# New orders for the steps of a two-layer graph attention kernel, with twelve instead of ten of a cycle's output sums on VectorE

## The chip, the core and the metric

The kernel runs on one core of one Trainium2 chip. The core has five engines that work at the same time, each through its own queue of instructions in order: TensorE (PE in the profile: matmuls, with PEld for the loading of the stationary operand), VectorE (DVE), ScalarE (ACT), GpSimd (POOL) and SyncE (SP, which here issues the DMA transfers). The metric is the device time of one execution in microseconds (us); the time of a kernel is the median over its runs.

## The reference

All data is float32: `x` is 128 batches x 128 agents x 512 features, `adj` is 128 batches x 128 x 128, zeros and ones. Two layers follow one another, each with a residual and a layer norm.

```python
def _L0_gnn_ref(inputs, adj, Wq, bq, Wk, bk, Wv, bv, Wo, bo):   # 8 heads of 64
    q = (inputs @ Wq + bq).reshape(bs, n, N_HEADS, HEAD_DIM)     # k and v likewise
    logits = jnp.einsum('bqhd,bkhd->bhqk', q, k) / np.sqrt(HEAD_DIM)
    logits = jnp.where((adj > 0)[:, None, :, :], logits, NEG_INF)
    attn = jax.nn.softmax(logits, axis=-1)
    out = jnp.einsum('bhqk,bkhd->bqhd', attn, v).reshape(bs, n, EMBED_DIM)
    return jax.nn.relu(out @ Wo + bo)

def _L1_gnn_ref(h, W, a, adj):
    Wh = jnp.matmul(h, W)
    e = _leaky((Wh @ a1)[:, :, None] + (Wh @ a2)[:, None, :])
    e = jnp.where(adj > 0, e, -9e15)
    attention = jax.nn.softmax(e, axis=1)
    return _leaky(jnp.einsum('bij,bjf->bif', attention, Wh))

x = _layernorm(x + _L0_gnn_ref(x, adj, ...))
x = _layernorm(x + _L1_gnn_ref(x, W1, a, adj))
```

## The kernel before

**Products.** The 512 x 512 products are done by the scheme of Strassen and Winograd: seven products of quarter-size blocks (`p1` to `p7`) in place of eight, with sums of blocks before and after (`strassen`, with the order of its pieces in `ORDER`). The projections to Q, K and V work on a group of four batches and use the scheme twice, nested. Each of the three is done in two *rounds*, one for each part of the inner scheme: an even round with four inner products, an odd round with three. Six rounds make a group (`c % 6`: 0 and 1 for Q, 2 and 3 for K, 4 and 5 for V). The products of layer 0 with Wo and of layer 1 with W1 work on a pair of batches and use the scheme once. W1 carries a 257th column for the edge scores.

**Orders.** No scheduler chooses the order of instructions. Under `tc.manual_schedule` every engine gets its instructions in the order in which the Python code issues them, and that order is written out as lists of tokens: `BEGIN` for the first six batches, four lists in `STEADY` for batch step t = 6 to 123 (the list t % 4), and `PLAN` for the end. A token names a step; its instructions are appended to the queues of the engines that it uses. A queue runs strictly in order, and each instruction waits at the head of its queue until its inputs are there and its output buffer is free. So the lists fix what stands behind what on each engine, while the order between engines comes from the data. SP issues all transfers of the steady part, also in list order, and an issue takes some 0.48 us on SP in the trace.

A steady list's token is a job, a dot and a step of it. The jobs:

- `f` and `s`: the softmax of layer 0 for two batches. `scores` (PE, L874), `add` (the mask, DVE L888), `reduce` (row maxima, DVE L897), `exp.i.j` (heads i and j, ACT L908), `reciprocals` (DVE L918), `divide` (ACT L922), `store` and `fetch` (the probabilities go to DRAM and come back with 32 x 32 blocks in place, L929 and L935, into `paz`), `transpose` (DVE L941, `pa<-paz`), `attend` (PE L954, `p_oT`), `copy` (ACT L969), `sum.n` (POOL L522 to L525). Both batches of a pair have their scores in an even list and attend in the odd list after it.
- `z`: layer 0's product with Wo for a pair, `p1` to `p7` (PE L800), `t0`, `t2`, `t3` (ACT copies, L811), `by`, `bw` (bias copies into the PSUM bank, ACT L821), `c11`, `c12` (DVE L1058), `c22` (DVE, a first add at L1062 and a residual at L1046), `c21` (L1046), `stats` (DVE L1002, L1004), `rstd` (POOL L1008, L1010), `apply` (DVE L1023), `store` (L1082). `g` and `p` are the same pair one and two lists later: `apply`, `store`, `fetch_both`, `transpose` (DVE L425) and `sum.n` (POOL).
- `w`: layer 1's product with W1 for a pair (PE L800, 257 columns wide), with its copies (ACT L811, and L1143 for `c21`) and adds (DVE L1145).
- `e`, `n`, `v`: layer 1's edges. `v.senders`, `v.store`, `v.fetch` send the outer sums through DRAM (L1176, L1251, L1261); `e.turn_blocks` (DVE L1186), `e.add` (ACT L1190), `e.maxima` (DVE L1196), `e.exp` (ACT L1200), `e.divide` (DVE L1204, L1205), `e.product` (PE L1210), `e.copy` (ACT L1217). One list later the batch is `n`: `residual` (DVE L1220), `stats`, `rstd`, `apply`, `store`.
- `m`: `masks`, `cast` (ACT L849), `mask` (DVE L852), `residuals` (L447), `x_pair` and `x_one` (loads of x, L420), `turn` (its 32 x 32 transposes, DVE L425), `sum.n` (the outer sums of x for the next group, POOL L522 to L525).

Tokens without a job are steps of the projections, and take the next one due:

- `h`: one outer product of a round, four or three matmuls (`split_step`, matmuls at L680). It queues up what reads its PSUM bank.
- `a`: the next of those copies, ACT (`copy_out`, L693, L696, L699). `d`: the next of those adds, DVE (L714).
- `k`: the next of the sums that finish a round (`combine`, the add at L730), on POOL; `k.v`: the same on VectorE.
- `i.s1a` to `i.s4b`: a sum of the inner scheme on x, on POOL, with `.v` on VectorE (L499).
- `q`: the load of the next weight block into a ring of four (`fetch_until`, L633).

Tiles with one buffer tie steps together: `paz`, the cells of a round, the three PSUM banks of the projections (`st_y`, `st_w`, `st_x`) and the five banks that all other products share. This loop runs the lists:

```python
        for token in STEADY[t % GROUP].split():
            if not common(token, g if t % GROUP else g + 1):
                name, method, *numbers = token.split(".")
                getattr(jobs[name], method)(*map(int, numbers))
```

Of the kernel before, what the change touches and what calls it, by code (L numbers as in the profile page):

```python
# [23 lines left out]
    y.order.3 y.q.0.0 y.order.2 b0.masks y.q.1.0 y.rows.2 y.rows.3 b4.load.1 b6.load.0  # L24
    b5.load.2 w.bias b2.masks y.q.2.0 y.q.2.1 y.q.1.1 y.oq.1 y.k.3 y.k.1 y.k.2 b4.turn
    b1.cast y.q.3.0 y.q.0.1 b0.cast y.oq.2 b7.load.1 y.q.3.1 b1.mask wk.build.0 b6.turn
    b5.turn wk.build.1 b3.cast b0.mask wk.build.2 wk.build.3 y.ok.2 b2.cast wq.scale.0
    y.oq.0 wq.scale.1 wq.scale.2 y.ok.1 y.ok.3 wq.scale.3 wk.build.4 wk.build.5 y.k.0 y.ok.0
    y.oq.3 s0.scores wk.build.6 b7.turn wk.build.7 b2.mask b3.mask s1.scores g1.0 g1.2
    b9.load.0 b8.load.2 w.halve wq.build.0 wq.build.1 wk.store.0 wq.build.2 s0.add.1  # L30
    s0.add.0 g1.1 i1.s1b b4.masks s0.reduce s1.add.0 s1.add.1 i1.s2b g1.3 wk.store.1
    s0.exp.0.1 s0.exp.6.7 b4.cast s0.exp.4.5 i1.s1a.v wk.store.2 y.v.1 wk.store.3 s0.exp.2.3
    b5.cast q q y.v.0 y.v.2 y.v.3 i1.s3a.v s1.reduce wq.build.4 s0.reciprocals.0
    s0.reciprocals.1 s0.divide.4.5 s0.divide.2.3 i1.s2a wq.build.3 i1.s4a.v wq.build.5
    s1.exp.5.6 s0.divide.0.1 h s1.exp.7 s1.exp.3.4 s0.divide.6.7 y.ov.0 s1.exp.0.1 y.ov.2
# [12 lines left out]
    s1.attend h g2.2 k h z0.p1 d w.w1_sum.2 k.v s1.copy a s3.reciprocals.1 d s1.sum.0
    s1.sum.2 h h z0.p2 b5.mask w.w1_sum.0 s1.sum.1 s3.exp.0.1 a z1.bw a b6.cast z0.t0
    s3.reciprocals.0 h z0.p6 h s3.divide.3.4 s3.divide.7 d w.w1_sum.1 s3.divide.5.6 z0.t2  # L50
    s3.divide.0.1 s3.divide.2 a h z0.p7 z0.p5 h q s2.fetch q w.w1_sum.3 w.block.3 w.w1_sum.6
# [14 lines left out]
    z0.transpose.1 d s5.transpose h h h z1.c12 z1.stats.0 z1.apply.1 d b13.load.0  # L66
    w.w1_block.0 i2.s4b w.w1_block.1 q q h s5.attend z1.rstd.0 z0.sum.0 a a s4.copy s5.copy
    z0.sum.1 z0.sum.2 w.w1_block.2 k w.w1_block.3 z0.sum.3 s5.sum.0 s5.sum.2 s5.sum.1 k k
    s5.sum.3 b13.turn z1.store.1
"""  # L70

STEADY = {
# [95 lines left out]
def kernel(  # L168
# [155 lines left out]
    wk = Weights(late)  # L324
# [1430 lines left out]
```

## Time and profile before

| | |
|---|---|
| median of 3 runs | 2299.22 us (2293.2, 2299.22, 2300.85) |
| the profiled execution: time, span | 2296.74 us, 2295.0 us |
| mean granted PE clock | 0.997 |
| PE busy | 2250.2 us, 98% |
| DVE busy | 2031.0 us, 89% |
| ACT busy | 1654.5 us, 72% |
| POOL busy | 1538.4 us, 67% |
| DMA | 540.80 MB, mean 236 GB/s |

The span is the profiled execution's time from its first to its last event, and its own time lies 1.74 us above it. A share is the busy time of an engine by the span; the shares of engines overlap. A row of waits names the engine and line that waited, the engine and line that released it, the sum, the times and the longest. In the timelines a start is in microseconds from the start of the span, and an idle time ahead of a row stands in brackets with its releaser. The steady lists run from about 174.5 us to 2199.5 us. Steps of the next stage are already mixed in at both ends.

### The profile page before, as it was taken

How to read it: one execution, taken by the hardware profiler on the slowest of the kernel's cores; microseconds unless marked ns; L12 is line 12 of the kernel's file. 1: busy time of each engine (PE TensorE's matmuls, PEld its weight loads, DVE VectorE, ACT ScalarE, POOL GpSimd, SP SyncE). 2: the span in 40 equal slices, each digit the busy share in tenths (PEclk: the TensorE clock that was granted, in tenths of full speed). 3: DMA queues.
4: the chain of work that ended last, by engine and by line, in shares of the span. 5: the costliest groups of instructions: out<-in, count | busy, mean ns of one | idle time of the engine just before them, and what ended most of it. 6: DMA issues, size and time to landing. Idle time of an engine off the chain costs nothing.

```text
span 2295.0 us, 52710 instructions
## 1 busy us (share of the span) xinstructions
PE 2250.2 (98%) x17228; PEld 2015.3 (88%) x17228; DVE 2031.0 (89%) x4140; ACT 1654.5 (72%) x5955; POOL 1538.4 (67%) x1782
## 2 busy tenths in 40 slices
PE   9999999999999999999999999999999999999998
PEld 5888998898898999998988998989898989888885
DVE  5879999999999999999999898999899998989877
ACT  3757677687676786776776777877767767768786
POOL 2656766667776677676667666677666776666656
PEclk9999999999999999999999999999999999999999
DMA  8977888788888888787878888778878888877764
GB/s 231 279 203 231 239 240 246 237 236 238 237 239 248 240 234 241 238 249 243 234 234 248 234 245 243 237 239 239 236 247 233 237 240 243 242 238 232 220 212 143
DMA packets 516594, 540.80 MB, mean 236 GB/s; under 512 B 100568, under 2 KB 394336, under 8 KB 516320
## 3 DMA queue, kind: packets, MB, share of 16 engines
q1 hardware_dynamic: 516000, 537.17, 79.4%
q8 instruction: 137, 2.24, 0.4%
q14 instruction: 137, 1.12, 0.2%
q10 hardware_dynamic: 320, 0.26, 0.0%
HBM read 388.96 MB, written 148.31 MB: 234 GB/s over the span
## 4 chain that ended last, share of the span: by engine, by line
PE 58%; DVE 17%; POOL 8%; DMA 8%; ACT 3%; issue 2%; SPq 2%; DVEq 0%; POOLq 0%; ACTq 0%
PE st_y L680 19%; PE p_y L800 13%; PE st_w L680 8%; PE p_w L800 7%; PE st_x L680 4%; DMA paz<-pa_dram 3%; DVE nmax L897 3%; DVE pa L888 3%; PE p_h L1210 2%; PE p_x L800 2%; POOL out_Q L730 2%; POOL rstd L1010 2%; POOL out_K L730 2%; PE lg L874 2%; ACT pa L908 1%
## 5 line engine op out<-in xcount | busy, mean ns | idle before, releaser
L908 ACT ACTIVATE pa<-pa,nmax 128x128 f32<-128x128 f32 x1000 | 391.9, 397 | 52.8 <-DVE nmax L897 51.8
L922 ACT ACTIVATE pa<-pa,rs 128x128 f32<-128x128 f32 x1000 | 326.6, 395 | 1.8 <-DVE rs L918 1.8
L969 ACT ACTIVATE arena<-p_oT,b_cols 128x128 f32<-128x128 f32 x504 | 141.2, 382 | 155.2 <-PE p_oT L954 155.1
L524 POOL TENSOR_TENSOR x1S<-x1T 128x256 f32<-128x256 f32 x62 | 48.7, 786 | 245.6 <-PE st_y L680 237.3
L1010 POOL TENSOR_TENSOR rstd<-ve,mhalf 128x1 f32<-128x1 f32 x256 | 189.7, 741 | 21.3
L693 ACT COPY cells<-st_y 128x384 f32<-128x384 f32 x279 | 132.6, 475 | 86.9 <-PE st_y L680 70.8
L908 ACT ACTIVATION_READ_ACCUMULATOR pa<-pa,nmax 128x1 f32 x1000 | 192.9, 193 | 0.0
L941 DVE STREAM_TRANSPOSE pa<-paz 128x1024 f32<-128x1024 f32 x125 | 154.8, 1238 | 19.3 <-DMA paz<-pa_dram 12.4
L1002 DVE BATCH_NORM_STATS2 st<-arena 128x6 f32<-128x512 f32 x248 | 168.8, 681 | 1.2
L888 DVE TENSOR_TENSOR pa<-lg,mf 128x512 f32<-128x512 f32 x250 | 164.3, 678 | 5.7 <-PE lg L874 5.7
L1008 POOL TENSOR_SCALAR ve<-mv 128x1 f32<-128x1 f32 x256 | 82.2, 321 | 129.3 <-DVE mv L1004 127.7
L714 DVE TENSOR_TENSOR cells<-st_w,cells 128x384 f32<-128x384 f32 (+1 forms) x217 | 123.2, 568 | 44.2 <-ACT cells L693 41.6
L897 DVE TENSOR_REDUCE nmax<-pa 128x8 f32<-128x1024 f32 x125 | 152.4, 1219 | 4.1
L1023 DVE TENSOR_SCALAR arena<-arena,mv,rstd 128x512 f32<-128x512 f32 x239 | 143.7, 601 | 14.0 <-POOL rstd L1010 14.0
L730 POOL TENSOR_TENSOR out_Q<-out_Q,cells 128x512 f32<-128x512 f32 x91 | 131.6, 1447 | 15.4 <-DVE out_Q L730 9.9
L954 PE MATMUL p_oT<-pa,out_V 128*64 128x128 f32 x2000 | 127.6, 278 | 9.2 <-DVE pa L941 9.1
L800 PE MATMUL p_y<-wo_w,x1S 128*128 128x257 f32 x496 | 131.1, 386 | 3.9 <-ACT arena L811 0.2
L874 PE MATMUL lg<-out_K,out_Q 64*128 64x128 f32 x2048 | 133.8, 280 | 0.7 <-ACT out_K L1394 0.7
L800 PE MATMUL p_y<-wo_w,x1T 128*128 128x257 f32 x496 | 134.4, 393 | 0.0
L874 PEld LDWEIGHTS lg<-out_K,out_Q 64*128 64x128 f32 x2048 | 120.8, 189 | 12.8 <-issue 10.4
L730 POOL TENSOR_TENSOR out_K<-out_K 128x512 f32<-128x512 f32 x32 | 53.7, 1681 | 115.6 <-PE st_x L680 107.0
L800 PE MATMUL p_y<-wo_w,oS 128*128 128x256 f32 x504 | 129.7, 380 | 0.5 <-ACT y L811 0.5
(300 smaller groups left out, 7845.7 us busy)
## 6 DMA issues: line engine op xcount, KB each, us to landing
paz<-pa_dram SPq DMA_DIRECT2D x504, 128.0 KB, 3.6
pa_dram<-pa SPq DMA_DIRECT2D x125, 512.0 KB, 3.1
w_n<-wk SPq DMA_DIRECT2D x93, 512.0 KB, 4.7
w_n<-wv SPq DMA_DIRECT2D x93, 512.0 KB, 5.5
w_n<-wk SPq DMA_DIRECT2D x93, 384.0 KB, 4.1
w_n<-wv SPq DMA_DIRECT2D x93, 384.0 KB, 4.6
x_dram<-arena SPq DMA_DIRECT2D x128, 256.0 KB, 3.3
xz<-x_dram SPq DMA_DIRECT2D x240, 128.0 KB, 3.4
```

Of the source, the lines that this page charges most:

```text
L680: nc.tensor.matmul(p[:, index, :], lhs, rhs, start=start and index == 0, stop=True, skip_group_check=True,)
L730: (by or engine).tensor_add(*(t(n) for t, n in (dst, left, right)))
L800: nc.tensor.matmul(p[:, :width], xs()[n][:, kc, :], w[:, PLACE[n], kc, :], start=start and kc == 0, stop=True, skip_group_check=True,)
L874: nc.tensor.matmul(self.lg[r][:, c, :], q[rows, 2 * (b % 2) + c % 2, c // 2, :], k[rows, 2 * (b % 2) + c % 2, c // 2, :], start=c == 0, st ...
L888: nc.vector.tensor_add(by_head[:, r * NC : (r + 1) * NC], self.lg[r].rearrange("p c (b k) -> p c b k", b=4), mf.unsqueeze(1).to_broadcast( ...
L897: nc.vector.tensor_reduce(self.nmax, by_head, AX.XY, ALU.max, negate=True)
L908: nc.scalar.activation(self.pa[:, :, h, :], self.pa[:, :, h, :], AF.Exp, bias=self.nmax[:, h : h + 1], accum_out=self.sums[:, h : h + 1],)
L922: nc.scalar.activation(self.pa[:, :, h, :], self.pa[:, :, h, :], AF.Copy, scale=self.rs[:, h : h + 1])
L941: nc.vector.transpose(self.paT.rearrange("p h (a i) -> p a h i", i=32), self.paz.rearrange("p a (h k) -> p a h k", k=32),)
L1002: nc.vector.bn_stats(st, self.src)
L1010: nc.gpsimd.tensor_tensor(self.r, ve, mhalf, ALU.pow)
L1023: nc.vector.tensor_scalar(self.src, self.src, self.mv[:, 0:1], self.r, ALU.subtract, ALU.mult)
```

## The change

All six lists get a new order. Four batches (the four lists of `STEADY`) hold the same tokens as before, with these differences:

- twelve `k.v` and twelve `k` in place of ten and fourteen: list 0 has three as before, list 1 four (two before), list 2 three (two before), list 3 two (three before);
- four of the eight `i` sums on VectorE (`s1b`, `s2a`, `s3a`, `s3b`) in place of three (`s1a`, `s1b`, `s3a`);
- `s.exp.6.7` and `s.divide.2` stand at the end of list 0; before they stood at the start of list 1;
- one `h`, with a `q` and an `a`, changes lists.

In `BEGIN` fourteen sums are `k.v` and thirteen `k` (before twelve and fifteen), and fewer of the first group's `i` sums are on VectorE. In the whole program VectorE gets 85 instructions more and GpSimd 85 fewer; PE, ACT and SP have as many as before. `LayerZero.stats` makes the `Norm` object of a half when that half is asked for, no longer both at once; the instructions are the same.

```diff
 BEGIN = """
...
-    z1.c11 s5.reciprocals.1 i2.s3b k.v s5.divide.2 s5.divide.0.1 s5.divide.7 a z1.t3
-    s5.divide.3.4 s5.divide.5.6 d h h z1.p4 h z1.c22 w.w1_sum.7 w.w1_sum.11 h s4.fetch a
-    z1.c21 d a i2.s4a h z1.p3 s4.transpose w.w1_sum.10 b12.turn k k z1.stats.1 a z1.rstd.1
-    s5.store k.v k.v z0.fetch_both s5.fetch b14.load.2 h h s4.attend a d z0.transpose.0
-    z0.transpose.1 d s5.transpose h h h z1.c12 z1.stats.0 z1.apply.1 d b13.load.0
-    w.w1_block.0 i2.s4b w.w1_block.1 q q h s5.attend z1.rstd.0 z0.sum.0 a a s4.copy s5.copy
-    z0.sum.1 z0.sum.2 w.w1_block.2 k w.w1_block.3 z0.sum.3 s5.sum.0 s5.sum.2 s5.sum.1 k k
-    s5.sum.3 b13.turn z1.store.1
...
+    s5.exp.6.7 z1.t3 z0.store.0 q h i2.s3b s5.exp.2 a s4.store s5.exp.5 s5.exp.0.1 z1.p4 h
+    i2.s2a z0.fetch_both a s4.fetch d w.w1_sum.11 i2.s3a.v s5.reciprocals.1 h z1.c21
+    w.w1_block.0 s5.reciprocals.0 z1.c22 d h k.v s5.divide.2 s5.divide.7 s5.divide.3.4
+    s5.divide.0.1 h s5.divide.5.6 i2.s2b z1.p3 z1.p2 a a i2.s4a s5.store h z1.stats.1 q
+    b2.residual d z0.transpose.0 b12.turn h h s4.transpose z1.c11 w.w1_sum.10 k.v k.v k k
+    s5.fetch a h z0.transpose.1 z1.rstd.1 w.w1_block.1 s4.attend d z0.sum.0 z0.sum.2 a
+    b13.load.0 z1.c12 d i2.s4b w.w1_block.3 z0.sum.1 q q b14.load.2 h h h h s4.copy a a
+    z1.stats.0 s5.transpose s5.attend s5.copy d z1.rstd.0 z1.apply.1 k.v k.v z0.sum.3
+    s5.sum.0 b13.turn s5.sum.2 w.w1_block.2 z1.store.1 s5.sum.1 k s5.sum.3
 """
 STEADY = {
     0: """
-        f.scores m.sum.0 m.sum.2 e.turn_blocks k.v m.sum.1 k.v g.apply.0 n.residual f.add.1
-        f.add.0 s.scores q w.p1 h e.add f.reduce n.stats s.add.0 a w.t0 w.p6 h w.p2 m.turn d
-        e.maxima s.add.1 f.exp.2.3 w.t2 f.exp.0.1 f.exp.6.7 a f.exp.4.5 e.exp w.p7 h m.sum.3
-        s.reduce d h h f.reciprocals.0 e.divide i.s1a.v w.p5 g.store.0 m.residuals m.masks q
-        q n.rstd g.fetch_both w.t3 m.cast a f.divide.2.3 a f.divide.0.1 s.exp.0.1 q d w.c22
-        w.c11 f.reciprocals.1 w.p4 w.c21 v.senders f.divide.6.7 h w.p3 h h n.apply i.s1b.v
-        k.v g.transpose.1 m.mask g.transpose.0 n.store v.store f.divide.4.5 a s.exp.2
-        s.exp.3.4 s.exp.5 i.s2a f.store m.x_pair v.fetch f.fetch e.product h i.s2b a d
-        i.s3a.v s.reciprocals.0 w.c12 d e.copy k i.s3b
+        m.masks m.sum.0 f.scores m.sum.1 m.sum.2 k.v m.turn n.residual k.v g.apply.0
+        s.scores w.p1 g.store.0 q g.fetch_both w.p5 f.add.1 f.add.0 f.reduce s.add.0 s.add.1
+        e.turn_blocks q w.t0 w.p6 h q m.residuals f.exp.2.3 f.exp.0.1 h w.p2 h w.t2 e.add
+        f.reciprocals.0 f.exp.4.5 f.exp.6.7 a d n.stats f.reciprocals.1 w.c11 e.maxima d
+        w.p7 f.divide.0.1 f.divide.6.7 a w.t3 e.exp s.reduce h h f.divide.2.3 a f.divide.4.5
+        m.sum.3 n.rstd e.divide i.s1b.v d w.c22 n.apply i.s1a w.p4 h n.store f.store s.exp.2
+        w.c21 m.cast v.senders h s.exp.5 a v.store w.p3 s.exp.0.1 s.exp.3.4 h h e.product
+        i.s2a.v k.v g.transpose.0 g.transpose.1 s.reciprocals.0 m.x_pair k f.fetch v.fetch a
+        s.exp.6.7 s.divide.2 d m.mask i.s3a.v w.c12 d i.s2b e.copy i.s3b.v
     """,
     1: """
-        z.by s.divide.2 k.v n.residual h h h z.p1 i.s4b i.s4a a s.exp.6.7 z.t0 z.p2 z.p6 d
-        n.stats s.reciprocals.1 a s.divide.0.1 s.divide.3.4 s.divide.7 s.divide.5.6 k.v
-        e.turn_blocks m.turn z.c11 h h h s.store z.t2 e.add z.bw a e.maxima e.exp d
-        f.transpose n.rstd z.p5 z.p7 h q m.x_one s.fetch z.t3 e.divide z.c22 a m.cast z.p4
-        z.c21 n.apply n.store k h h z.p3 m.mask d h z.stats.1 z.c12 q k p.sum.0 k z.rstd.1
-        e.product h d f.attend a a e.copy q s.transpose s.attend z.stats.0 z.apply.1 f.copy
-        s.copy p.sum.2 k k p.sum.1 z.rstd.0 s.sum.0 p.sum.3 k z.store.1 s.sum.2 s.sum.1
-        s.sum.3
+        z.by m.cast n.residual z.p2 s.reciprocals.1 k.v n.stats p.sum.0 i.s4a h h h z.p1 h a
+        a d k.v h s.divide.0.1 s.divide.3.4 s.divide.5.6 s.divide.7 z.t0 h z.p6 z.bw a z.t2
+        m.turn k.v h d f.transpose z.c11 e.turn_blocks z.p7 a z.p5 d z.t3 z.c22 s.store z.p4
+        q e.add k k e.maxima m.mask s.fetch z.p3 h h p.sum.1 i.s4b n.rstd h n.apply e.exp a
+        e.divide z.c12 z.c21 a e.product h z.stats.1 d n.store f.attend q q m.x_one
+        s.transpose z.rstd.1 p.sum.2 s.attend z.stats.0 e.copy k.v z.apply.1 f.copy z.rstd.0
+        s.copy s.sum.0 k k s.sum.2 p.sum.3 s.sum.1 z.store.1 s.sum.3
     """,
     2: """
-        n.residual e.turn_blocks f.scores g.apply.0 f.add.0 f.add.1 s.scores w.p1 e.add w.t0
-        w.p2 w.p6 w.p5 f.reduce e.maxima k f.exp.4.5 e.exp w.t2 w.p7 f.exp.6.7 f.exp.2.3
-        w.t3 m.residuals g.store.0 q m.masks f.exp.0.1 h a h m.turn k.v n.stats e.divide
-        f.reciprocals.1 k.v m.x_one g.fetch_both s.add.1 f.divide.6.7 w.p4 n.rstd w.c21 h
-        n.apply d w.c11 m.cast h w.c22 f.reciprocals.0 v.senders a d e.product h h n.store
-        f.divide.0.1 s.add.0 w.p3 h a f.divide.4.5 s.reduce a f.divide.2.3 v.store q f.store
-        v.fetch e.copy w.c12 g.transpose.1 g.transpose.0 d m.mask
+        n.residual f.scores g.apply.0 e.turn_blocks s.scores w.p1 e.add w.p2 f.add.1 f.add.0
+        e.maxima f.reduce w.t0 e.exp g.store.0 m.masks q m.residuals w.p6 f.exp.6.7 w.p5
+        w.t2 f.exp.4.5 f.exp.0.1 w.p7 n.stats m.turn k.v f.reciprocals.1 k.v k.v w.c11 w.t3
+        h h f.exp.2.3 a w.p4 f.reciprocals.0 w.c22 d h h f.divide.4.5 n.rstd n.apply
+        e.divide w.c21 v.senders g.fetch_both m.x_one n.store w.p3 f.divide.6.7 s.add.0 a d
+        s.add.1 g.transpose.1 w.c12 s.reduce g.transpose.0 h e.product h f.divide.2.3 m.cast
+        f.divide.0.1 a a h h v.store q f.store e.copy d m.mask v.fetch
     """,
     3: """
-        z.bw p.sum.2 s.exp.2 z.by h z.p1 q s.exp.5 s.exp.6.7 a z.t0 s.exp.0.1 s.exp.3.4 h h
-        z.p6 n.residual n.stats m.turn d s.reciprocals.0 e.turn_blocks s.reciprocals.1 a k
-        p.sum.0 n.rstd k d z.t2 e.add s.divide.3.4 z.p2 h z.p5 h z.c11 s.divide.7 e.maxima
-        s.divide.5.6 s.divide.0.1 s.divide.2 k.v n.apply h m.cast a p.sum.1 z.p7 f.fetch h h
-        a z.t3 e.exp m.x_one q q d f.transpose e.divide z.c22 k k.v a z.p4 h h s.store z.p3
-        h a a k.v k q q h d z.c21 d z.stats.1 h a z.c12 p.sum.3 z.rstd.1 d e.product h h k
-        m.mask z.apply.1 z.stats.0 s.fetch n.store q q s.transpose f.attend s.attend f.copy
-        e.copy s.copy k z.rstd.0 s.sum.2 s.sum.0 s.sum.1 s.sum.3 z.store.1
+        m.turn n.residual k.v k z.by z.bw s.exp.3.4 a z.p1 h s.exp.2 s.exp.5 z.t0 s.exp.0.1
+        s.exp.6.7 d n.stats e.turn_blocks s.reciprocals.1 q h z.p6 a d s.reciprocals.0 h
+        z.p5 h z.t2 s.divide.5.6 s.divide.7 h z.p7 s.divide.0.1 s.divide.3.4 f.fetch d
+        f.transpose s.divide.2 a a q q s.store q q h m.cast z.t3 e.add h z.p4 h a k p.sum.0
+        n.rstd p.sum.2 h z.p2 z.c22 k n.apply k.v d z.c21 e.maxima h z.p3 a e.exp a z.c11 d
+        z.stats.1 e.divide z.c12 h h e.product h h s.fetch f.attend n.store k p.sum.1 k
+        z.rstd.1 d z.apply.1 q q z.store.1 q m.x_one z.stats.0 s.transpose s.attend a e.copy
+        f.copy s.copy a k k z.rstd.0 s.sum.0 p.sum.3 s.sum.2 s.sum.1 m.mask s.sum.3
     """,
 }
 ...
         def stats(self, h):
-            self.norms = self.norms or [
-                Norm(X1[2 * self.pair + n], self.on_scalar) for n in range(2)
-            ]
+            self.norms = self.norms or {}
+            self.norms[h] = Norm(X1[2 * self.pair + h], self.on_scalar)
             self.norms[h].stats()
 
         def rstd(self, h):
```

The list `PLAN` (453 tokens, not shown) is reordered throughout in the same way, with the same tokens.

## The prediction

> **What bounds the kernel now.** I began with the busy shares of the page, then took the windows to divide the span into stages, then what the matmul engine and its weight loads wait for inside the middle stage, and last the chain and the timelines at the places found. First the page and the windows (length, then the busy time of PE, PEld, DVE, ACT and POOL with instruction counts, the granted PE clock, the DMA share, GB/s):
>
> ```profile
> PE 2250.2 (98%) x17228; PEld 2015.3 (88%) x17228; DVE 2031.0 (89%) x4140; ACT 1654.5 (72%) x5955; POOL 1538.4 (67%) x1782
> ...
> 131.00:143.80 12.80, 9.31 (x70) 7.53 (x68) 6.45 (x13) 5.24 (x23) 11.68 (x16) 1.00 0.73 249
> 143.80:150.70 6.90, 6.01 (x27) 6.01 (x28) 4.43 (x9) 5.70 (x18) 0.00 (x0) 0.51 0.25 85
> ...
> 174.50:2133.20 1958.70, 1942.23 (x15178) 1760.96 (x15176) 1776.90 (x3613) 1437.51 (x5208) 1351.34 (x1540) 1.00 0.81 240
> ```
>
> PE is the bound. From 174.5 to 2133.2 us the step lists run 28 times over their four batches: 1958.7 / 28 = 69.95 us for a cycle. Start-to-start distances in the PE timeline give 0.89 us for a projection step of four products, 0.67 for one of three, 0.87 for a product of Wo or W1, 0.99 for a batch's scores, 0.93 to 0.97 for its attention, 0.86 for an edge product. 21 x 0.89 + 21 x 0.667 + 28 x 0.867 + 4 x 0.99 + 2 x (0.925 + 0.973) + 4 x 0.861 = 68.2 us. So a cycle holds about 1.75 us in which PE does no work, 28 x 1.75 = 49 us in all; the same sum leaves some 22 us in the begin and 9 in the end. The change adds and takes away no PE instruction: only these 80 us can be won, and any new wait of PE counts in full.
>
> The waits of PE and of its weight loads between 174.5 and 2199.5 us (sum, times, longest), and then the begin's longest, with the chain that leads to it:
>
> ```profile
> PE st_y L680 <- DVE out_K L714: 5.6, 12, 0.6
> PE p_oT L954 <- DVE pa L941: 4.4, 9, 1.0
> ...
> PEld p_y L800 <- ACT arena L811: 15.2, 29, 0.5
> PEld st_y L680 <- DVE out_K L714: 10.4, 12, 1.0
> PEld p_oT L954 <- DVE pa L941: 7.4, 12, 1.2
> PEld st_y L680 <- ACT cells L693: 6.7, 28, 0.2
> ```
>
> ```profile
> 135.06 1.05 POOL wo_w L260
> 136.11 0.69 POOL out_Q L730
> 136.80 1.49 POOL wo_w L261
> ...
> 140.95 1.36 POOL out_Q L730 x2
> ...
> 143.62 0.44 DVE out_Q L730
> ...
> 144.16 0.49 ACT cells L693
> ...
> 144.69 1.44 PE st_y L680 x5
> ```
>
> Distances between PE starts, less the work in between, price the same places: 0.61 us in 12 of 28 cycles where a projection step of list 3 waits for a DVE add into K (8.7 us with what follows it); 7.3 us where list 3's attention waits for DVE's transpose of the fetched probabilities, in 12 cycles; 0.28 us in every cycle, 10.8 with the step behind, at w.p7 in list 2, which waits for an ACT copy; 5.6 us around a step of list 0 that waits for ACT and DVE; some 11 us in scattered tenths. In the begin POOL works without a pause from 132.8 to 143.6, and PE waits 3.82 us.
>
> **The change, part by part.** Sums are made against the profiled execution, 2296.74 us (span 2295.0), 2.5 us or 0.1% under the median 2299.22.
>
> *Twelve sums on DVE, four inner sums instead of three.* Per cycle two 128x256 sums of Q and, net of swaps of equal size, one 128x384 inner sum leave POOL. The rows of the moved kinds:
>
> ```profile
> L730 POOL TENSOR_TENSOR out_Q<-out_Q x90: 711/727/736, 136.1 to 2170.1; 128x256 f32<-128x256 f32 x90
> L730 DVE TENSOR_TENSOR out_Q<-cells x30: 380/382/416, 136.8 to 2171.4; 128x256 f32<-128x256 f32 x30
> L730 DVE TENSOR_TENSOR out_V<-out_V,cells x31: 658/953/986, 124.2 to 2153.4; 128x512 f32<-128x512 f32 x31
> L730 POOL TENSOR_TENSOR out_K<-out_K x32: 1267/1718/1722, 91.6 to 2194.1; 128x512 f32<-128x512 f32 x32
> ```
>
> POOL: 2 x 0.70 + 1.35 = 2.7 us less of 45.3. DVE, by start-to-start distances (0.31 and 0.47): 2 x 0.31 + 0.47 = 1.1 us more, 60.8 to 61.9 of 69.95. Neither engine is full, so by itself this costs nothing; its cover is DVE's 8 us of slack per cycle, and it counts only in a stretch where PE waits for DVE. The last two rows show what meeting costs: the same sum takes 0.66 or 0.95 us on DVE, 1.27 or 1.72 on POOL. Three more meetings per cycle at +0.3 us bound it at 0.9 us of DVE time.
>
> The Trainium skill ("SBUF — State Buffer", Who interferes with whom) says that a DVE operation with two SBUF inputs and a GpSimd operation that reads SBUF exclude each other for the whole instruction. By that rule each sum moved to DVE could stand behind a whole POOL sum, 1.28 us by this case's rows, and 29 such in the tightest stretch below would be 37 us slower; the rows show +0.3, and go into my sum.
>
> *List 3, the transfers.* Before, DVE's x transpose m.turn stands right in front of the add into K that PE waits for, and the x load comes late. After, m.turn opens the list, the step's add has only it ahead, and the load is issued some 8 us before it is wanted, against landings of 3.3 us. The 8.7 us go. Bounds: 8.7 (all) and 0 (the load as late as now, since m.turn is also earlier). I take 8.7.
> The store of the probabilities comes about 0.4 us earlier and the fetch no longer stands behind the x load's four issues (0.48 us each on SP): about 2 us more room for a landing of 3.6 us. Waits here were 0.16 to 1.16 us, so most go; but DVE itself, back to back, ends this transpose about 67.5 us after the cycle's first scores, with 0.25 us to spare for PE. I take 5 of 7.3.
>
> *List 0.* e.turn_blocks moves behind the adds of the scores, so f.reduce ends at 3.6 to 4.2 us instead of 4.5 and the exponentials start earlier; the 0.24 us waits go: 4 of 5.6 (bounds 0 and 5.6). Moving s.exp.6.7 and s.divide.2 into this list changes ACT's order alone: 1 us of ACT work lies beside ACT's 18 us of idle time.
>
> *List 2.* w.t2 now stands behind one exponential instead of three; by the distances w.p7 waits 0.10 to 0.15 us, not 0.28: 4 of 10.8 are won. Bounds: 10 won, or, if f.reduce comes late, 0.6 us per wait, 9 lost.
>
> *List 1, the place that gets tighter.* z.p5 moves behind z.p7 and z.p3 stands 26.80 us of PE work after the cycle's first scores, before 28.36. z.p3 writes the bank that z.c22's first add (L1062) reads, and that add needs p5, which ends at 25.93. Before, DVE did this:
>
> ```profile
> 758.81 0.69 DVE L714 TENSOR_TENSOR out_Q<-st_x,out_Q 128x512 f32<-128x512 f32 x1 [0.69 <-PE st_x L680]
> 759.42 1.23 DVE L941 STREAM_TRANSPOSE pa<-paz 128x1024 f32<-128x1024 f32 x1
> ...
> 761.34 0.41 DVE L1062 TENSOR_TENSOR pr_t<-p_w,pr_t 128x256 f32<-128x256 f32 x1
> ```
>
> The scores started at 735.16, so the add ended at 26.6 and z.p3 had 1.8 us to spare. After, from s.reciprocals.0 at 15.85 to 16.4 us, DVE's list to that add is 0.08 + 0.47 + 0.10 + 0.66 + 0.33 + 0.47 + 0.47 + 0.60 + 0.08 + 0.61 + 0.82 + 0.55 + 0.61 + 1.25 + 0.61 + 0.60 + 1.16 + 0.32 + 0.20 + 0.60 + 0.41 = 11.0 us (mask, sums, statistics, x transpose, probabilities, adds): it ends at 26.85 to 27.4, if neither landing in it is late. z.p3 then waits 0.05 to 0.6 us; 0.9 with one meeting more, 0 if DVE gains as much before. Over 29 cycles: 0 to 26 us lost. I take 0.3, 8.7 us, the middle of the two ends.
>
> *Begin.* The two Q sums on DVE and later sums of z0 take about 5 us of POOL work out of the chain quoted; the wait was 3.82. Behind it PE ran at clock 0.51 for 6.9 us, about 3 us lost. 7 of 22 us go. Bounds: 10 (other begin waits too), and a loss of 3, since s1.attend stands 3.3 us of PE work later and all early steps are reordered.
> The Trainium skill ("TensorE: Matmul & The Clock Gate", What's actually happening) puts the gate at an idle window of about 3.4 us. The end's wait of 2.17 us (PE at 2201.89) was also followed by 3.5 us at 0.51 here, so the measurement decides. By the rule, a wait shortened to 2.5 us would save the 3 us; by this row not surely. If the wait goes, both say 7.
>
> *End.* Reordered throughout; its 9 us of waits are as many small ones. 0, bounds 4 either way.
> The lazy Norm of LayerZero.stats emits the same instructions, 0.
>
> Sum: -8.7 - 5 - 4 - 4 + 8.7 - 7 = -20 us: 2277 by the profiled execution, 2279 by the median; I say 2278.
>
> **Rivals.**
> *A, slower: list 1's z.p3 waits for DVE.* For it: 11.0 us of DVE work in a window of 10.4 to 11, two landings in it. Against: DVE enters earlier if list 0 runs freely. From 0.95 us per cycle (29 x 0.95 = 28) it eats all the gains named; at 1.3 us (the 0.6 and two meetings at +0.3) it is 38 lost: 2299 - 29 + 38 = 2308; to 2320 at 1.7.
> *B, only the begin gains:* small waits replace those removed, one for one, since the margins that I find elsewhere (0.1 us at z.p4, 0.25 to -0.15 at s.scores) are as thin as before's: 2299 - 7 = 2292.
> *C, it does not do what it says:* POOL's sums lay on PE's path in the begin alone, and if loads still land late because the queues are 80% busy, list 3's 14 us stay and a little is lost at z.p3: 2296.
>
> **How the numbers follow.** Mine 0.50 (own range 2257 to 2291: with every bound at its best 8.7 + 7.3 + 5.6 + 10 + 10 = 42 is won, with A's wait at its 0.6 only 11), A 0.24 (2303 to 2325), B 0.14 (2286 to 2298), C 0.12 (2288 to 2309). A change of 0.3%, 6.9 us, is about what a measurement of this kernel can tell from none: the bounds are 2292.3 and 2306.1. Faster: 0.48 of mine, 0.09 of B, 0.03 of C = 0.60. Slower: 0.21 of A, 0.04 of C and 0.01 of mine (list 2's bound) = 0.26. Same: the other 0.14. The range goes from the best bound, 2257, to 2316, the middle of A's upper half, and leaves out a tenth at either end.
>
> **What would show it.** Right: no PE wait for K at L714 in the middle, fewer than 5 at L941, no clock of 0.51 near 144 us, a cycle near 69.5 us. Wrong: a row for PE or PEld at L800 that waits for DVE L1062 in every cycle (A); the L714 and L941 rows unchanged (C); the middle as long as before with new rows in it (B).

## The result, and the profile after

The changed kernel takes 2264.44 us (median of 6 runs, 2259.86 to 2271.28), the kernel before 2300.69 us (6 runs, 2293.2 to 2309.01). The ratio is 0.9844, with a 95% interval of 0.9819 to 0.9869: 36 us faster. The forecast was 2278 us, with 2257 to 2316 as its range. The profiled execution after takes 2263.41 us, 33.3 us less than the one before.

The page and the windows of the changed kernel, cut where its stages begin (first scores of the step lists, first list 0, last list 0, first step of the end list; columns as before):

```profile
PE 2236.6 (99%) x17228; PEld 2015.0 (89%) x17228; DVE 2014.3 (89%) x4225; ACT 1661.6 (73%) x5955; POOL 1406.2 (62%) x1697
...
132.10:167.70 35.60, 34.91 (x278) 31.58 (x276) 27.70 (x57) 23.73 (x85) 18.64 (x23) 1.00 0.95 262
167.70:2102.70 1935.00, 1933.19 (x15178) 1763.29 (x15176) 1759.77 (x3697) 1443.89 (x5208) 1218.94 (x1457) 1.00 0.83 242
2102.70:2171.50 68.80, 67.37 (x528) 61.08 (x526) 61.40 (x129) 51.71 (x187) 43.46 (x52) 1.00 0.74 224
```

And the same stages of the kernel before:

```profile
131.00:174.50 43.50, 37.84 (x276) 34.23 (x274) 28.57 (x59) 24.25 (x85) 24.75 (x30) 0.92 0.74 220
174.50:2133.20 1958.70, 1942.23 (x15178) 1760.96 (x15176) 1776.90 (x3613) 1437.51 (x5208) 1351.34 (x1540) 1.00 0.81 240
2133.20:2203.70 70.50, 68.21 (x532) 61.56 (x528) 61.20 (x125) 51.34 (x185) 48.38 (x55) 0.99 0.72 223
```

The first list 0 starts 6.8 us earlier (167.7, not 174.5), 28 cycles take 23.7 us less (69.11 us each, not 69.95), what follows to the end list 1.7, and the end list 1.2 (2261.6 - 2171.5 = 90.1, not 91.3): together 33.4 us. VectorE is busy for less time, 1759.8 against 1776.9 us, with 84 instructions more in these 28 cycles. GpSimd loses 132 us there, of which the moved sums are 28 x 2.7 = 76.

Inside the cycles the lost time can be put down to steps. I take the distance from the start of each PE step to that of the next, less the lower quartile of the distances of the same kind (the same two kinds of step behind each other), and sum it by list over 28 cycles:

| lost PE time in 28 cycles, us | list 0 | list 1 | list 2 | list 3 |
|---|---|---|---|---|
| before | 10.4 | 0.5 | 14.0 | 18.2 |
| after | 10.4 | 3.7 | 3.2 | 2.2 |

What PE and its weight loads still wait for in the step lists of the changed kernel, from 174.5 us to 2199.5 us (lines are two to four smaller than before):

```profile
PE p_oT L952 <- DVE pa L939: 1.9, 2, 1.4
PE st_x L678 <- DVE cells L712: 0.4, 1, 0.4
...
PEld st_w L678 <- ACT cells L697: 6.9, 29, 0.2
PEld st_w L678 <- DVE pa L886: 6.7, 28, 0.2
PEld p_y L798 <- ACT pr_t L809: 5.7, 28, 0.7
PEld p_oT L952 <- DVE pa L939: 3.5, 6, 1.7
```

The rows for the add into K and for the copy behind w.p7 (PEld, 10.4 and 15.2 us before) are gone. The rows of some 0.2 us per wait are waits of weight loads that PE's matmuls hide: the PE steps behind them start at most 0.02 us late on average. Before had one of them too.

### The profile page after: what moved, and what is told of

Its sections match the earlier page's. It is cut to its first block, busy times and chain, and to the rows that moved or that the text cites. A ratio compares the mean times of both kernels' runs of the same rounds, so it can differ in the third digit from the quotient of the medians.

```text
span 2261.6 us, 52550 instructions
## 1 busy us (share of the span) xinstructions
PE 2236.6 (99%) x17228; PEld 2015.0 (89%) x17228; DVE 2014.3 (89%) x4225; ACT 1661.6 (73%) x5955; POOL 1406.2 (62%) x1697
## 4 chain that ended last, share of the span: by engine, by line
PE 89%; DMA 4%; DVE 4%; ACT 1%; SPq 1%; issue 1%; POOL 0%; POOLq 0%; DVEq 0%; ACTq 0%
PE st_y L678 24%; PE p_y L798 19%; PE st_w L678 12%; PE p_w L798 9%; PE st_x L678 6%; PE lg L872 6%; PE p_oT L952 5%; PE p_x L798 5%; PE p_h L1207 4%; DMA adj<-in_adj_dram 1%; DMA paz<-pa_dram 1%; DMA w_n<-wv 0%; SPq L933 0%; ACT pa L920 0%; DVE pa L939 0%
## 5 line engine op out<-in xcount | busy, mean ns | idle before, releaser
L728 POOL TENSOR_TENSOR out_Q<-out_Q,cells 128x512 f32<-128x512 f32 x92 | 116.2, 1277 | 297.4 <-DVE out_Q L728 297.4
L1008 POOL TENSOR_TENSOR rstd<-ve,mhalf 128x1 f32<-128x1 f32 x256 | 161.4, 631 | 21.3
L1006 POOL TENSOR_SCALAR ve<-mv 128x1 f32<-128x1 f32 x256 | 76.1, 297 | 147.7 <-DVE mv L1002 145.0
L872 PE MATMUL lg<-out_K,out_Q 64*128 64x128 f32 x2048 | 139.6, 281 | 0.7 <-ACT out_K L1391 0.7
L728 POOL TENSOR_TENSOR out_K<-out_K 128x512 f32<-128x512 f32 x62 | 79.1, 1275 | 91.1 <-DVE out_K L728 91.1
L1214 ACT ACTIVATE arena<-p_h 128x512 f32<-128x512 f32 x120 | 71.9, 599 | 83.8 <-DMA out_dram<-arena 60.2
L798 PE MATMUL p_y<-wo_w,arena 128*128 128x256 f32 x504 | 131.3, 383 | 0.9 <-ACT pr_t L809 0.9
L1021 DVE TENSOR_SCALAR arena<-arena,mv,rstd 128x512 f32<-128x512 f32 x239 | 131.2, 549 | 0.6 <-POOL rstd L1008 0.6
```

The source lines that it names most:

```text
L728: (by or engine).tensor_add(*(t(n) for t, n in (dst, left, right)))
L798: nc.tensor.matmul(p[:, :width], xs()[n][:, kc, :], w[:, PLACE[n], kc, :], start=start and kc == 0, stop=True, skip_group_check=True,)
L872: nc.tensor.matmul(self.lg[r][:, c, :], q[rows, 2 * (b % 2) + c % 2, c // 2, :], k[rows, 2 * (b % 2) + c % 2, c // 2, :], start=c == 0, st ...
L1008: nc.gpsimd.tensor_tensor(self.r, ve, mhalf, ALU.pow)
```

## Experiments

The first four runs change the kernel before, one thing each. If the forecast's reasons hold, each wins a part of the gain. The columns of waits are as above.

**The add ahead of the x transpose (list 3).**

```diff
-        z.p6 n.residual n.stats m.turn d s.reciprocals.0 e.turn_blocks
+        z.p6 n.residual n.stats d m.turn s.reciprocals.0 e.turn_blocks
```

> The kernel before, with one pair of tokens exchanged in list 3: the add d stands ahead of the x transpose m.turn on VectorE. If the 0.61 us waits of PE for that add (12 of 28 cycles, 8.7 us with the step behind) come from m.turn waiting for its load at the head of VectorE's queue, they vanish and the profiled execution is 8 to 9 us shorter than before's, about 2288. Rival: the wait comes from the DVE queue being late as a whole, or the transpose in its later place delays the next add that PE needs; then the waits only change their row, and the time stays within 3 us of before's.

Measured: 2302.31 us against 2302.07 of the kernel before, ratio 0.9994 (0.9977 to 1.0012). The step behind z.p2 is never late, but the one behind z.p7 is, by 0.40 us in 21 cycles (8.5 us): the rival holds. VectorE's whole list was late there and the wait only found the next add. The add had not waited for a load. The 21 cycles are exactly those in which n.residual, ahead of it on VectorE, takes 1.81 us and not 0.68; the last four runs come back to that.

**The load behind the fetch (list 3).**

```diff
-        a z.t3 e.exp m.x_one q q d f.transpose e.divide z.c22 k k.v a z.p4 h h s.store z.p3
+        a z.t3 e.exp q q d f.transpose e.divide z.c22 k k.v a z.p4 h h s.store z.p3
...
-        m.mask z.apply.1 z.stats.0 s.fetch n.store
+        m.mask z.apply.1 z.stats.0 s.fetch m.x_one n.store
```

> The kernel before, with the load m.x_one of list 3 moved behind s.fetch on SP, past f.transpose, s.store and the loads q. If the late landing of the probabilities comes from the queue that stands ahead of their fetch, the waits of p_oT for the transpose in list 3 (6.6 us of steps that start late, 12 cycles) fall below 2 us, and the time by 4 to 6 us. Rival: the fetch waits for s.store's landing and not for SP; then the waits stay at 5 to 8 us and the time stays within 2 us. If x comes late for list 0's transpose instead, the time grows by up to 10.

Measured: 2305.09, ratio 1.0007 (0.9989 to 1.0026). s.attend loses 6.8 us (6.6 before). The fetch is issued 6.49 us ahead of f.attend (median of its four issues), before 6.45, and its last part lands 0.51 us ahead, before 0.54: SP had not held it up, and the rival holds.

**The copy ahead of the exponential (list 2).**

```diff
-        w.p2 w.p6 w.p5 f.reduce e.maxima k f.exp.4.5 e.exp w.t2 w.p7
+        w.p2 w.p6 w.p5 f.reduce e.maxima k f.exp.4.5 w.t2 e.exp w.p7
```

> The kernel before, with w.t2 one place earlier in list 2, ahead of e.exp on ScalarE. The wait of w.p7 (0.28 us, every cycle) is for that copy. If ScalarE's order sets it, the 7.9 us and the 2.9 behind them go at least to a third: 7 to 10 us shorter. Rival: the copy is late because f.exp.4.5 ahead of it waits for f.reduce on VectorE; then e.exp's 0.4 us is all that can be won and the wait stays at 0.1 us or more, 3 to 5 us shorter, or none.

Measured: 2303.48, ratio 0.9998 (0.998 to 1.0016). The wait of w.p7 falls from 7.9 to 0.6 us, but the step behind w.p4 now starts 0.15 us late in nearly every cycle, 4.3 us, and the next one adds 2.9. List 2 loses 12.8 us (14.0). The order of these two alone moves the wait to the next copy.

**Three sums of the begin on VectorE.**

```diff
-    z0.sum.1 z0.sum.2 w.w1_block.2 k w.w1_block.3 z0.sum.3 s5.sum.0 s5.sum.2 s5.sum.1 k k
+    z0.sum.1 z0.sum.2 w.w1_block.2 k.v w.w1_block.3 z0.sum.3 s5.sum.0 s5.sum.2 s5.sum.1 k.v k.v
```

> The kernel before, with the last three sums k of BEGIN as k.v, on VectorE (two sums of 128x256 and one that follows them). GpSimd loses 3 x 0.69 us of its unbroken stretch up to 143.6 us. If that stretch sets the 3.82 us wait at 144.7 us and the half clock behind it, the wait falls to 2 us or less, the clock stays at 1.0, and the begin is 4 to 6 us shorter. Rival: the wait comes from the order of steps around it (copies on ScalarE, the fetch of the pair's rows), then it stays above 3 us and the time within 2 us of before's.

Measured: 2300.44, ratio 0.9984 (0.9967 to 1.0001). The clock stays at 1.00 from 131 to 175 us, but the begin is not shorter: the first list 0 starts at 175.8 us (before 174.5), and in this execution a wait of 2.1 us at 111 us is followed by 3.4 us at half clock. PE's waits from 131 to 150 us (the lines of this kernel are one smaller):

```profile
PE p_x L799 <- DVE pa L887: 3.0, 1, 3.0
PE st_w L679 <- DVE cells L713: 0.6, 1, 0.6
```

The wait for the copy (3.8 us) is gone, so GpSimd's stretch did set it; in its place PE waits 3.0 us for VectorE. There the three sums, which need 0.31 us each where they are alone, take 2.15 us in one row:

```profile
137.87 2.15 DVE L729 TENSOR_TENSOR out_Q<-out_Q 128x256 f32<-128x256 f32 x3
139.94 0.70 DVE L424 STREAM_TRANSPOSE xT<-xz 128x512 f32<-128x512 f32 x1
140.57 1.37 DVE L1022 TENSOR_SCALAR arena<-arena,mv,rstd 128x512 f32<-128x512 f32 x1
```

The next four change the changed kernel. On their chip the kernel before has a median of 2310.92 us, so they are read by their ratios to it; the changed kernel's is 0.9844.

**Ten sums again.**

```diff
-        e.copy k.v z.apply.1
+        e.copy k z.apply.1
...
-        w.t2 f.exp.4.5 f.exp.0.1 w.p7 n.stats m.turn k.v f.reciprocals.1 k.v k.v w.c11 w.t3
+        w.t2 f.exp.4.5 f.exp.0.1 w.p7 n.stats m.turn k.v f.reciprocals.1 k.v k w.c11 w.t3
...
-        i.s2b e.copy i.s3b.v
+        i.s2b e.copy i.s3b
```

> The changed kernel, with ten of a cycle's sums on VectorE as before (one in list 1 and one in list 2 go back to GpSimd) and the inner sum s3b back on GpSimd. If the moved sums lie off PE's path, the time stays within 4 us of the changed kernel's, 2261 to 2269, and VectorE is 1 us less busy per cycle, GpSimd 2.7 us more. Rival: GpSimd's relief is what the steady gain rests on; then new waits for sums L728 or for operands of x appear and the time grows by 10 us or more, towards 2280.

Measured: 2272.73, ratio 0.9834 (0.9817 to 0.9851). Not to be told from 0.9844, so the rival's 10 us and more are refuted: which engine does these three sums is worth less than the two intervals together show, some 0.3% or 7 us. GpSimd is busy 1298.2 us in the 28 cycles and not 1218.9, 2.8 us more per cycle as expected; VectorE is busy 1756.0 and not 1759.8, 0.1 us less per cycle where 1 was expected.

**The sum ahead of the residual (list 0).**

```diff
-        m.masks m.sum.0 f.scores m.sum.1 m.sum.2 k.v m.turn n.residual k.v g.apply.0
+        m.masks m.sum.0 f.scores m.sum.1 m.sum.2 k.v m.turn k.v n.residual g.apply.0
```

> The changed kernel, with n.residual behind the second k.v at the head of list 0 on VectorE. The scores of s now start 0.15 to 0.2 us late in every cycle (5.5 us in all between s.scores and w.p1, 1.7 between f.scores and s.scores). If they wait for that sum, which comes 0.6 us earlier here, the two places fall below 1.5 us together and the time by 4 to 6 us, to about 2259. Rival: they wait for ScalarE's copies of the attention before; then nothing changes, 2262 to 2267.

Measured: 2300.99, ratio 0.9949 (0.993 to 0.9969). The two places fall from 7.3 us to 0.4, as expected, and the kernel is about 1% slower than the changed one, which neither side foresaw. List 1 loses 41.1 us. One addition on VectorE shows why. First the changed kernel, VectorE and GpSimd at the head of a list 1:

```profile
738.36 0.68 DVE L1217 TENSOR_TENSOR arena<-arena 128x512 f32<-128x512 f32 x1
738.97 0.17 DVE L916 RECIPROCAL rs<-sums 128x4 f32<-128x4 f32 x1
739.05 0.66 DVE L728 TENSOR_TENSOR out_V<-out_V 128x512 f32<-128x512 f32 x1
739.63 0.68 DVE L1000 BATCH_NORM_STATS2 st<-arena 128x6 f32<-128x512 f32 x1
```

```profile
739.01 1.83 POOL L497 TENSOR_TENSOR inner_s<-xT,inner_s 128x512 f32<-128x512 f32 x1 [2.38 <-PE st_w L678]
```

And the same place of this experiment:

```profile
754.72 0.68 DVE L1217 TENSOR_TENSOR arena<-arena 128x512 f32<-128x512 f32 x1
755.32 0.17 DVE L916 RECIPROCAL rs<-sums 128x4 f32<-128x4 f32 x1
755.40 1.67 DVE L728 TENSOR_TENSOR out_V<-out_V 128x512 f32<-128x512 f32 x1
757.00 0.68 DVE L1000 BATCH_NORM_STATS2 st<-arena 128x6 f32<-128x512 f32 x1
```

```profile
755.17 1.35 POOL L497 TENSOR_TENSOR inner_s<-xT,inner_s 128x512 f32<-128x512 f32 x1 [2.20 <-PE st_w L678]
```

The same two sums, and in both cases they do not run together. Where they start within 0.04 us of each other (GpSimd's start is the earlier by the record), VectorE takes its 0.66 us and GpSimd's takes 1.83 instead of 1.35. Where GpSimd is 0.23 us ahead, VectorE's takes 1.67, that is 755.17 + 1.35 = 756.52, and then its own 0.55. This happens in 1 of 29 cycles of the changed kernel's profile and in 29 of 29 here: 29 x 1.0 us of VectorE's time, in the stretch that ends at z.c22. Counted from the cycle's first scores, GpSimd's sum, which PE releases, starts 0.11 us earlier here in these two cycles and VectorE's 0.08 us later (0.07 and 0.13 by the medians): that decides who is first.

**More work ahead of z.c22.**

```diff
-        z.p7 a z.p5 d z.t3 z.c22 s.store z.p4
+        z.p7 a z.p5 d z.t3 n.stats z.c22 s.store z.p4
```

> The changed kernel with more work: n.stats is done a second time in list 1, right ahead of z.c22 on VectorE (0.82 us there by the distances of its two instructions; the second result is used, it is the same). If z.p3 of list 1 stands at the very edge, as its 0.05 us per cycle in the changed kernel says, nearly all of that shows at z.p3: 0.7 to 0.85 us per cycle, 29 cycles, 20 to 25 us slower than the changed kernel. Rival: other slack takes it up, VectorE catching up inside the stretch; then under 8 us.

Measured: 2303.54, ratio 0.9963 (0.9949 to 0.9977): about 1.2% above the changed kernel, 27 us. z.p3 starts 0.73 to 0.80 us late in 26 of 28 cycles and 1.1 in the other two, 21.8 us, and the step behind it adds 2.9. The edge is where the expectation put it. Lost races of the kind shown above, in 7 cycles, add some 10 us to list 1 in this profile.

**The old begin.** The list `BEGIN` of before in the changed kernel.

> The changed kernel with the begin list of before; step lists and end list are the new ones. If the begin's gain of 6.8 us up to the first list 0 belongs to its order alone, the wait near 144 us with the half clock comes back and the time is 6 to 8 us longer than the changed kernel's, about 2271. Rival: the new step lists in the first cycle remove the wait, whatever the begin; then within 3 us.

Measured: 2271.39, ratio 0.9836 (0.9801 to 0.987), no difference from the changed kernel that can be told; with 8 us to either side, the times alone don't decide between the two sides. In its profile the first list 0 starts at 170.5 us (before 174.5, after 167.7), and PE has no wait above 0.6 us in the lists ahead of it. So the long wait goes with the new list 2, the first list that runs; by these single profiles 4.0 of the 6.8 us are the step lists' and 2.8 the begin's. The split is rough: the first list 0 starts at 172.8 to 175.1 us in the five profiles with the old begin and the old list 2, and at 166.5 to 168.9 in the seven with both new; and the profile of this run has 3.4 us at half clock at 112 us, behind a wait of 2.3 us, which the changed kernel's lacks.

The last four test the new reason, that VectorE and GpSimd exclude each other for a whole instruction, on one chip (the kernel before: 2307.49 us).

**GpSimd kept from meeting n.residual (the kernel before, list 3).**

```diff
-        z.p6 n.residual n.stats m.turn d s.reciprocals.0 e.turn_blocks s.reciprocals.1 a k
-        p.sum.0 n.rstd k d z.t2
+        z.p6 n.residual n.stats m.turn d s.reciprocals.0 e.turn_blocks s.reciprocals.1 a n.rstd k
+        p.sum.0 k d z.t2
```

> The kernel before, with n.rstd ahead of the first k of list 3 on GpSimd; VectorE's list is untouched. In the traces that sum k and VectorE's n.residual start within 0.02 us of each other; where k is first, n.residual takes 1.81 us and not 0.68, and PE waits 0.61 us later. Here GpSimd stands behind n.stats, which comes after n.residual, so the two can't meet. If their meeting is the cause, n.residual takes 0.68 us in all 28 cycles and the waits of the step behind z.p2 fall from 5 to 12 us below 1 us; the execution gets 6 to 12 us shorter unless the later k makes a new wait. Rival: the cause is the x load or the length of VectorE's list; then the waits stay, or come back at z.p7.

Measured: 2295.45, ratio 0.9946 (0.9925 to 0.9967): 12 us faster than the kernel before, by an exchange in GpSimd's queue alone. n.residual takes 0.68 us in list 3 in all 28 cycles, and the step behind z.p2 loses nothing in any of them. The timelines of the kernel before show what was taken away, first in a cycle where PE waits (VectorE, then GpSimd):

```profile
574.49 1.81 DVE L1220 TENSOR_TENSOR arena<-arena 128x512 f32<-128x512 f32 x1
576.34 0.69 DVE L1002 BATCH_NORM_STATS2 st<-arena 128x6 f32<-128x512 f32 x1
577.07 0.18 DVE L1004 BATCH_NORM_AGGREGATE mv<-st 128x2 f32<-128x6 f32 x1
577.24 0.71 DVE L425 STREAM_TRANSPOSE xT<-xz 128x512 f32<-128x512 f32 x1
577.88 0.65 DVE L714 TENSOR_TENSOR out_K<-st_x,out_K 128x512 f32<-128x512 f32 x1
```

```profile
574.48 1.27 POOL L730 TENSOR_TENSOR out_Q<-out_Q,cells 128x512 f32<-128x512 f32 x1
```

and in one where it doesn't:

```profile
505.00 0.68 DVE L1220 TENSOR_TENSOR arena<-arena 128x512 f32<-128x512 f32 x1
505.71 0.69 DVE L1002 BATCH_NORM_STATS2 st<-arena 128x6 f32<-128x512 f32 x1
```

```profile
504.98 1.83 POOL L730 TENSOR_TENSOR out_Q<-out_Q,cells 128x512 f32<-128x512 f32 x1
```

The x transpose at 577.24 starts as soon as the statistics ahead of it are done, so no load was late. n.residual and the sum start within 0.02 us of each other, and whoever wins makes the other wait: 1.13 us for VectorE, 0.55 for GpSimd. The recorded starts don't tell who wins: GpSimd's is the earlier by 0.01 to 0.02 us in all 28 cycles, and VectorE wins 16. Counted from list 2's first scores, the instructions ahead of the two in list 3 start at the same times on both engines, within 0.01 us by their medians, in the cycles of either kind. In three profiles with list 3 as it was (the kernel before and the third and fourth run) PE waits there in 12, 18 and 9 of 28 cycles, exactly those in which n.residual takes 1.81 us. One new meeting took the old one's place: n.apply, 0.54 us alone, takes 0.95 us more in 26 of 28 cycles and 0.41 in two (before, 0.41 in 14). PE loses less by it: some 15 us in list 3 in this profile, by the measure of the table above, against 18.2 in that of the kernel before and some 30 and 24 in those of the third and fourth run.

**A later sum of x1S (the changed kernel, list 1), and both exchanges.**

```diff
-        z.by m.cast n.residual z.p2 s.reciprocals.1 k.v n.stats p.sum.0 i.s4a h h h z.p1 h a
+        z.by m.cast n.residual z.p2 s.reciprocals.1 k.v n.stats i.s4a h h h z.p1 h a
...
-        q e.add k k e.maxima m.mask s.fetch z.p3 h h p.sum.1 i.s4b n.rstd h
+        q e.add k k p.sum.0 e.maxima m.mask s.fetch z.p3 h h i.s4b n.rstd p.sum.1 h
```

> The changed kernel, with GpSimd's p.sum.0 of list 1 behind the two sums k, and p.sum.1 behind n.rstd. In the changed kernel p.sum.0 starts 0.02 us ahead of VectorE's i.s3a.v, which then takes 1.26 us and not 0.68 in every cycle. If meetings on the two engines are what delays VectorE here, i.s3a.v falls to 0.68, the stretch up to z.c22 is 0.5 us shorter, the first k.v of list 1 starts well before i.s4a in every cycle, and the 1.5 us of waits at z.p3 go: 1.5 to 3 us shorter than the changed kernel on the same chip. Rival: another GpSimd sum meets VectorE in its place, and the time stays or grows by up to 30.

> The same, and n.residual behind the second k.v of list 0 as well, the exchange that alone cost about 1 us per cycle. If that cost came only from the k.v of list 1 standing behind i.s4a on GpSimd (1.67 us and not 0.65), it is gone here, the scores of s are no longer late, and the time is 5 to 9 us below the changed kernel's, about 2257 where that has 2264. Rival: VectorE's list is the bound there whatever is exchanged; then z.p3 of list 1 waits 0.2 us more per cycle and the time is that of the changed kernel or above.

> The changed kernel itself, as the measure for the two beside it on one chip: about 0.984 of the kernel before.

Measured: 2280.19 (ratio 0.9885, 0.9851 to 0.9918), 2279.5 (0.9884, 0.9855 to 0.9913), and 2271.09 for the changed kernel (0.9843, 0.982 to 0.9867). Neither is better; the rival of the first holds. i.s3a.v does fall from 1.26 to 0.68 us, but VectorE's first k.v of list 1 still loses in 8 cycles and, with both exchanges, in 12 (4 in the changed kernel on this chip). In the same cycles i.s1b.v of list 0 has lost 1.1 us to i.s1a on GpSimd, so the late start is handed down. In the first, z.c22 loses 0.43 us in 19 cycles. No order tried here is faster than the changed kernel by more than these intervals.

## Why the prediction was right, point by point

- *The bound.* PE is the bound, its work did not change, and the gain came out of its waits: right.
- *Twelve sums on DVE*, costed at nothing: not contradicted by the run with ten, within the 7 us that it can tell. The term inside it, a meeting at +0.3 us, was mis-sized. I read it from medians of rows that mix shapes of overlap. A meeting costs up to the whole of the other engine's instruction: 1.0 us (k.v, 0.66 to 1.67) and 1.13 us (n.residual) on VectorE, 0.5 us and more on GpSimd. The Trainium skill ("SBUF — State Buffer", Who interferes with whom) says just that, an exclusive lock for the instruction, taken by whoever issues first. I weighed the rule and went by the rows. These runs agree with the lock; they agree with the order too where the starts lie 0.23 us apart (GpSimd ahead, 29 of 29 cycles), and can't show it for starts within 0.05 us, where the engine recorded second often wins.
- *List 3, the transfers*: -13.7 forecast, -16.0 measured (18.2 to 2.2), but the step "the x load comes late" is false, so that the 8.7 us came out is luck. The waits for the add into K were lost races between n.residual and a sum on GpSimd; the new order puts that sum behind the k.v that follows n.residual, and the waits of GpSimd show it standing there in all cycles, so they do not meet. For the attention, the store is issued 0.4 us earlier as forecast and the fetch 0.5 us (not the 2 us of the text), its last landing moves from 0.54 to 1.42 us ahead of f.attend (medians of the 22 cycles in which the trace has it), and 5.2 of 6.6 us go. That the fetch stood behind the x load's issues is refuted; whether the earlier store does it all was not isolated.
  The row of GpSimd's waits after:

```profile
POOL out_Q L728 <- DVE out_Q L728: 279.2, 29, 9.9
```

- *List 0*: -4 forecast, 0 measured. The 5.6 us did go, and 7.3 us came at the scores of s, a place that the text gave a margin of 0.25 to -0.15 and no price. f.reduce ends 3.8 us after the first scores, as forecast. Before, it ended at 4.5 us in the 16 cycles in which the step is late and at 3.9 in the other 12, and in the traces this difference again starts where VectorE and GpSimd are at work together. VectorE's g.apply waits for GpSimd's z.rstd.0 (L1008 and L1010), which takes 0.66 and 0.98 us where VectorE's two sums k.v start first, and 0.21 and 0.56 where it is ahead of them. A late cycle, then one on time (VectorE, then GpSimd; first scores at 804.21 and 874.09):

```profile
803.10 1.56 DVE L730 TENSOR_TENSOR out_K<-out_K,cells 128x512 f32<-128x512 f32 x2
805.11 0.55 DVE L1023 TENSOR_SCALAR arena<-arena,mv,rstd 128x512 f32<-128x512 f32 x1 [0.45 <-POOL rstd L1010]
```

```profile
803.34 0.66 POOL L1008 TENSOR_SCALAR ve<-mv 128x1 f32<-128x1 f32 x1
804.09 0.98 POOL L1010 TENSOR_TENSOR rstd<-ve,mhalf 128x1 f32<-128x1 f32 x1
```

```profile
873.12 1.40 DVE L730 TENSOR_TENSOR out_K<-out_K,cells 128x512 f32<-128x512 f32 x2
874.44 0.54 DVE L1023 TENSOR_SCALAR arena<-arena,mv,rstd 128x512 f32<-128x512 f32 x1
```

```profile
872.77 0.21 POOL L1008 TENSOR_SCALAR ve<-mv 128x1 f32<-128x1 f32 x1
873.07 0.56 POOL L1010 TENSOR_TENSOR rstd<-ve,mhalf 128x1 f32<-128x1 f32 x1
```

  No run exchanges these steps alone, so this is read from the traces and not tested.
- *List 2*: -4 forecast, -10.8 measured. The wait is gone whole. Moving the one copy does not do it. The traces point to another move, e.maxima ahead of f.reduce on VectorE: e.exp then runs 3.43 us after the list's first scores, in time in which ScalarE sat idle before, and no longer at 5.06, right ahead of w.t2. ScalarE's last copy of the product (w.c21) starts at 8.84 us and not 9.24; with the one copy moved it stays at 9.24. ScalarE's e.exp and w.t2, before and after (list 2's first scores at 768.93 and 753.77):

```profile
773.99 0.39 ACT L1200 ACTIVATE att<-att,nmax 128x128 f32<-128x128 f32 x1
...
774.38 0.35 ACT L811 COPY arena<-p_y 128x257 f32<-128x257 f32 x1
```

```profile
757.20 0.40 ACT L1197 ACTIVATE att<-att,nmax 128x128 f32<-128x128 f32 x1
...
758.67 0.37 ACT L809 COPY arena<-p_y 128x257 f32<-128x257 f32 x1
```

  That move was not tried alone.
- *List 1, the place that gets tighter*: +8.7 forecast, +3.2 measured, of which z.p3 is 1.5 (0.05 us per cycle, the low end of the 0 to 0.6). Rival A's mechanism is real: 0.8 us more on VectorE there costs 0.73 to 0.80 per cycle at z.p3. The sum of 11.0 us for the stretch was too small, 11.64 measured, mostly because i.s3a.v takes 1.26 us and not 0.66: in every cycle it meets GpSimd's p.sum.0, here 0.02 us ahead of it (VectorE, then GpSimd):

```profile
735.91 1.26 DVE L497 TENSOR_TENSOR xT<-xT 128x512 f32<-128x512 f32 x1
```

```profile
735.89 0.74 POOL L520 TENSOR_TENSOR x1S<-x1T 128x256 f32<-128x256 f32 x1
```

  Three things made up for it. VectorE enters the stretch at 15.43 us and not at 15.85 to 16.4, so the add ends at 27.07, inside the forecast; the other race, k.v against i.s4a, is won in 28 of 29 cycles; and PE itself comes to z.p3 at 27.2 us and not 26.80, with the 0.4 us per cycle that list 0 still loses. So the misses of lists 0 and 1 belong together, and the low end was in part luck.
- *Begin*: -7 forecast, -6.8 measured, with no clock below full in that stage after. The wait is GpSimd's doing, as the text had it, but it goes with the new list 2 as well as with the begin. The 3 us for the half clock behind it hold for the profile of before alone: the first, second, third and ninth runs have the same wait, 3.7 to 3.8 us, and a mean clock of 0.96, 0.96, 0.96 and 1.00 from 131 to 175 us, where before has 0.92.
- *End*: 0 forecast; -1.2, and -1.7 in the cycle and a half ahead of it.

The sum was -20, the profiles give -33.4. Of the 13 us between them most is list 2 (6.8) and list 1 (5.5), then the end and what leads to it (2.9) and list 3 (2.3); list 0 went 4 the other way. PE's waits as the source of the gain were right; that the sizes came near in list 3 was not due to the reasons given. Rival B, only the begin, fell with the 23.7 us of the cycles, rival C with the 16 of list 3.

## What to carry to other kernels

When a wait comes in some cycles and not in others, with a fixed size, lay one cycle of each kind side by side on all engines: a row whose duration differs (0.68 and 1.81 us) is the place to test for the cause; a queue that is merely late is not. In a schedule written by hand, look for two-operand instructions on VectorE and GpSimd that become ready at the same time, and hold one of them behind something else in its queue. A change of 0.2 us elsewhere can turn such a race in every cycle, so an exchange of two steps must be measured whole.

## What was not expected of the hardware

- An addition of two SBUF operands on VectorE and a GpSimd addition do not overlap: 0.66 or 1.67 us on VectorE, 1.35 or 1.83 on GpSimd, by a difference of 0.2 us in their starts. Within 0.03 us either can win, whatever the record of their starts says: VectorE 16 of 28 meetings of n.residual before, and none of 28 of i.s3a.v after.
- It reaches small instructions too: the mask's 128x128 VectorE instruction, 0.18 us in one place (L850 after), takes 0.56 in another (L852 before, 574.01 us), where a GpSimd sum runs from 573.79 to 574.52.
- Races that turn from cycle to cycle go with the spread between executions: the changed kernel's profile with 1 lost k.v has 69.11 us per cycle, that with 4 has 69.45, and with 9 (the old begin, same step lists) 69.76. These are three profiles, not all of one chip.
- Over 28 cycles, durations above the fastest twentieth of the same line and form (counted from 0.12 us on) sum to 71 us on VectorE and 157 us on GpSimd before, 36 and 72 us after.
